# A gated mLSTM and mixture-of-experts layer: small second products queued behind other products, and four held groups of tiles in place of three

## The chip, the core and the metric

The kernel runs on one core of a Trainium2 chip. The metric is the device time of one execution in microseconds (us). Engines are named as in the profile: PE is the matrix engine, PEld its weight loads, DVE the vector engine, ACT the scalar engine, POOL the GpSimd engine, and SP the engine whose queue issues most DMA transfers. All data are fp32.

## The reference, cut to what matters

There are 8 sequences of 512 tokens, so 4096 tokens of width 1024, which the kernel cuts into 32 tiles of 128 tokens.

```python
x = x + tanh(g_xattn) * mlstm(layernorm(x), ctx, ctx, Wi, bi, Wf, bf, ln_scale)  # 16 heads of 64
x = x + tanh(g_ffn)   * ffn(layernorm(x), router_w, gate_w, up_w, down_w, shared_*)

# ffn, for T tokens of width 1024, 16 experts, the two best of each token
router_logits = flat @ router_w.T
topk_w, topk_idx = top_k(softmax(router_logits), 2);  topk_w /= sum(topk_w)
shared = (silu(flat @ shared_gate_w) * (flat @ shared_up_w)) @ shared_down_w    # hidden 1024
routed = sum over the two experts of topk_w * (silu(x @ gate_w[e]) * (x @ up_w[e])) @ down_w[e]  # hidden 512
output = shared + routed
```

In `mlstm`, an input gate and a forget gate per head come from products of the query, key and value rows with `Wi` and `Wf`. Their running sums and maxima along the sequence give a matrix of weights `d` for each head. The scores `q k` are multiplied by it, the values are summed with it, and each head is normalised.

## The kernel before

The kernel has two stages. The first goes over the 32 tiles in order. For each tile it does the attention, stores the normalised row for the experts (`y_d`, and transposed `yT_d`), routes the tile to its experts, and in between, as fill for PE, computes the shared expert of earlier tiles. The second stage runs "jobs" of up to 512 rows and a hidden width of 512: one for each of the 16 experts, and then two (the two halves of the hidden width of 1024) for each *held* group of four tiles. Held tiles are the last `4 * HELD` tiles, whose shared expert is left to the second stage. A job there multiplies in Winograd's form, seven products of quarter blocks in place of eight (`Step`, `down_tiles`), which the fill of the first stage does not.

**The loop of the first stage** (`for i in range(1, NT)`) prepares tile i + 1 while it finishes tile i and the rows of tile i - 1. On PE it issues, in the order of the program: transposes of the queries of tile i + 1 (`prep_queries`, tile `qT`), the first half of the scores of tile i (`scores(i, 0)`), transposes of the keys (`prep_keys`), fill, the gate products of tile i + 1 (`prep_gates`), the second half of the scores (`scores(i, 1)`), fill, half of the values, transposes of the finished rows of tile i - 1 (`turn_rows`), fill, router products of tile i - 1 (`finish_route`), the rest of the values, the growth of the state (`grow`), a small transpose (`prep_columns`), and fill. The first four tiles of the loop differ only in the share of fill.

**Two-step products.** `in_groups` spreads a narrow product over four groups of 32 columns of the array (tile `pp`), ACT copies the result to SBUF (tile `parts`, line 413), and a second product with the constant `sums` adds the four groups: tile `pg` (line 451) for the gates, tile `pl` (line 687) for the router. PE cannot start the second product before the copy is done.

**After pg** comes a chain for tile i + 1: ACT copies `f` (line 458), DVE works through about fifteen small operations with three visits to ACT (lines 459 to 488, ending in `nm`), and SP stores `nm` and `e` to memory and reads them back broadcast, as `d` (1 MB) and `eb` (512 KB). POOL cuts `d` to a triangle (line 522), DVE takes `decay` from `eb` (line 528) and scales `eb`, and ACT takes the exponentials of `d` (line 564), which the scores of the next turn of the loop are multiplied with (line 580). The row norms (`row_stats`, `inverse_deviation`, `normed`) go from DVE to POOL, which computes the inverse deviation (`rstd`, lines 114 and 117), and back to DVE (`row`, line 418).

**Routing.** Tiles are routed in groups of four (the last four in groups of 2, 1 and 1). When the last tile of a group has its logits, `route_group` makes one-hot rows on DVE (`hot`, `both`, `upto`), has PE add them up over the partitions (tile `pn`, lines 731 to 733, the "rank products"), computes the slots on DVE (`slots_i`, line 755), and has POOL write the eight columns of row numbers to a table in memory with indirect DMAs (line 758).

**Fill.** `shared_units` cuts the shared expert of a pair of tiles into 12 units: 8 chunks of the hidden width (line 247, 16 products of 256 columns) and 4 projections down (line 263, 8 products of 512 columns). `fill(n)` adds n to what is owed and issues whole units until the debt is paid. Weights for a chunk (two tiles of 512 KB) are streamed by SP two units ahead. From the fifth tile on, each of the four calls of a turn asks for

```python
each = (6 * (NT - 4 * HELD) - 1 - 3 * FIRST - RESERVE) / (4 * (NT - 1 - FIRST))
```

with NT = 32, FIRST = 4 and RESERVE = 8: the units of the tiles that are not held, spread over the loop, with 8 kept for the end of the stage. With HELD = 3 this is 0.917.

**Order on the engines.** The program is traced in this order, and a scheduler then builds the queue of each engine from it, by the program's order and what it takes to be ready. Each engine works off its queue in order. `tc.issue_after(ins)` keeps what is traced under it behind `ins` in the queue of the engine of `ins`, without a wait of its own.

Of the kernel before, what the change touches and what calls it, by code (L numbers as in the profile page):

```python
# [23 lines left out]
NE = 16  # L24
F = 512
NS = S // P
NC = D // P
# [5 lines left out]
MAIN = 512  # L33
REST = 64
PAIRS = 5
HELD = 3
SINGLE = 2
RESERVE = 8
FIRST = 4
# [3 lines left out]
def flamingo_layer(  # L43
# [20 lines left out]
    nc = tc.nc  # L64
    B = x.shape[0]
    T = B * S
    NT = T // P
# [135 lines left out]
    units: deque[Unit] = deque()  # L203

    owed = 0.0

    def fill(n: float = 1):
        nonlocal owed
        owed += n
        while owed > 1e-6 and units:  # L210
            unit = units.popleft()
            owed -= unit.cost
            unit.ready()
            for k in range(min(2, len(units))):
                units[k].ready()
            unit.run()
        if not units:
            owed = 0.0

    def shared_units(tiles, near=None):  # L220

        st: dict = {}
        n = len(tiles) * P

        def load_y():
            if near is not None:
                st["yT"] = near
                return
            st["yT"] = sh.tile([P, NC, 2 * P], F32, tag="yT2", name="sh_yT")
            for t, i in enumerate(tiles):  # L230
                nc.sync.dma_start(
                    st["yT"][:, :, t * P : (t + 1) * P], yT_d[i].rearrange("p (c t) -> p c t", t=P)
                )

        def load_chunk(k: int):
            if k == 0:
                load_y()
            st[k] = stream(k)

        def chunk(k: int):  # L240
            if k == 0:
                st["hT"] = sh.tile([P, 2 * NFC, 2 * P], F32, tag="hT2", name="sh_hT")
            wg, wu = st.pop(k)
            pg = ps.tile([P, 2, 2 * P], F32, tag="g", name="pgu")
            for half, w in enumerate((wg, wu)):
                for c in range(NC):
                    nc.tensor.matmul(  # L247
                        pg[:, half, :n], lhsT=w[:, c, :], rhs=st["yT"][:, c, :n],
                        start=(c == 0), stop=(c == NC - 1),
                    )  # L250
            act = sh.tile([P, 2 * P], F32, tag="act", name="sh_act", bufs=2)
            nc.scalar.activation(act[:, :n], pg[:, 0, :n], AF.Silu)
            nc.vector.tensor_mul(st["hT"][:, k, :n], act[:, :n], pg[:, 1, :n])

        def load_row(t: int):
            st["row", t] = sh.tile([P, D], F32, tag="base", name="sh_base", bufs=2)
            nc.sync.dma_start(st["row", t], x1_d[tiles[t]])

        def project_down(t: int, half: int):
            cols = slice(half * 512, (half + 1) * 512)  # L260
            po = ps.tile([P, 512], F32, tag="o", name="pso")
            for k in range(2 * NFC):
                nc.tensor.matmul(  # L263
                    po, lhsT=st["hT"][:, k, t * P : (t + 1) * P], rhs=sh_down[:, k, cols],
                    start=(k == 0), stop=(k == 2 * NFC - 1),
                )
            row = st["row", t]
            nc.vector.scalar_tensor_tensor(row[:, cols], po, tgf, row[:, cols], ALU.mult, ALU.add)
            if half == 1:
                nc.sync.dma_start(acc_d[tiles[t] * P : (tiles[t] + 1) * P, :], row)  # L270

        cost = len(tiles) / 2
        us = [Unit(lambda k=k: chunk(k), lambda k=k: load_chunk(k), cost) for k in range(2 * NFC)]
        for t in range(len(tiles)):
            us.append(Unit(lambda t=t: project_down(t, 0), lambda t=t: load_row(t)))
            us.append(Unit(lambda t=t: project_down(t, 1)))
        return us

    early = ExitStack()
    sh = early.enter_context(tc.tile_pool(name="sh", bufs=1, side="right"))  # L280
# [17 lines left out]
    with ExitStack() as actx:  # L298
# [37 lines left out]
        before_p = ac.tile([P, P], F32, name="before_p")  # L336
# [107 lines left out]
            q.kT = wk.tile([P, NC, P], F32, tag="kT", name="kT")  # L444
            transposed(q.kT, lambda c: q.kv[:, c * P : (c + 1) * P], [nc.vector.tensor_copy] * 2)

        def prep_gates(i: int):
            q, last, first = toks[i], i % NS == NS - 1, i % NS == 0
            parts = in_groups(wgt, lambda c: (q.qT if c < NC else q.kT)[:, c % NC, :], 2 * NC)
            pg = ps.tile([48, P], F32, tag="tr", name="pg")  # L450
            nc.tensor.matmul(pg, lhsT=sums, rhs=parts, start=True, stop=True)

            def row(name, bufs=2):
                return gt.tile([NH, P], F32, tag=name, name=name, bufs=bufs)
# [111 lines left out]
        def scores(i: int, g: int):  # L566

            q = toks[i]
            banks = [ps.tile([P, 4, P], F32, tag="a", name="psc") for _ in range(2)]
            for k in range(8):  # L570
                h = 8 * g + k
                lanes = slice((h % 2) * DH, (h % 2 + 1) * DH)
                nc.tensor.matmul(
                    banks[h % 2][:, k // 2, :], lhsT=q.kT[lanes, h // 2, :],
                    rhs=q.qT[lanes, h // 2, :], start=True, stop=True,
                )
            d = q.d.rearrange("p (h a) s -> p a h s", a=2)
            for hh in range(2):
                half = d[:, hh, 4 * g : 4 * g + 4, :]
                q.scored = nc.vector.scalar_tensor_tensor(  # L580
                    half, banks[hh], DH**-0.5, half, ALU.mult, ALU.mult
                ).ins

        def values(i: int, g: int):

# [5 lines left out]
            for k in range(2):  # L591
                c = 2 * g + k
                if not first:
                    nc.tensor.matmul(
                        pav[:, 2 * k : 2 * k + 2, :].rearrange("p a e -> p (a e)"),
                        lhsT=q.eb[:, c, :], rhs=state[:, c, :], start=True, stop=False,
                    )
                for hh in range(2):
                    h = 2 * c + hh
                    nc.tensor.matmul(  # L600
                        pav[:, 2 * k + hh, :], lhsT=q.d[:, h, :], rhs=q.v[:, h, :],
                        start=first, stop=first or hh == 1,
                    )
            heads = slice(4 * g, 4 * g + 4)
            nc.scalar.copy(q.u[:, heads, :], pav)
            nc.scalar.activation(q.sq[:, heads, :], pav[:, :, 0:DH], AF.Square)

        def grow(i: int):

# [70 lines left out]
                tiles = [i] if alone else [i - 1, i]  # L680
                units.extend(shared_units(tiles, near=yT if i == 0 else None))

        def finish_route(i: int):
            q = toks[i]
            parts = in_groups(rwT, lambda c: q.yT[:, c, :], NC)
            pl = ps.tile([P, NE], F32, tag="o", name="pl")
            nc.tensor.matmul(pl, lhsT=parts, rhs=sums[:, 0:NE], start=True, stop=True)
            r = group_of(i)
            k = i - r.first
            nc.vector.tensor_copy(r.logits[:, k, :], pl)  # L690
# [22 lines left out]
        def route_group(first: int):  # L713
# [3 lines left out]
            n = r.n  # L717
# [9 lines left out]
            upto = uptos[first // 4 % 2]  # L727
            for k in range(n):
                nc.vector.tensor_add(upto[:, k + 1, :], upto[:, k, :], both[:, k, :])
            pn = ps.tile([P, n + 1, NE], F32, tag="o", name="pn")  # L730
            nc.tensor.matmul(pn[:, :n, :], lhsT=before_p, rhs=both, start=True, stop=False)
            nc.tensor.matmul(pn[:, :n, :], lhsT=ones_p, rhs=upto[:, :n, :], start=False, stop=True)
            nc.tensor.matmul(pn[:, n, :], lhsT=ones_p, rhs=upto[:, n, :], start=True, stop=True)
            pos = sm.tile([P, n, NE], F32, tag="pos", name="pos", bufs=2)
# [51 lines left out]
        with tc.issue_after(normed.last):  # L786
            prep_gate_weights()
            prep_values(0)
        prep_gates(0)
        prep_columns(0)  # L790
        with tc.issue_after(normed.last):
# [12 lines left out]
        finish_rows(0)  # L804
        prep_queries(1)
        prep_keys(1)
        prep_gates(1)
        grow(0)
        turn_rows(0)
# [4 lines left out]
        load_x(2)  # L814
        prep_columns(1)
        load_kv(2)
        finish_route(0)
        fill()
        prep_norm(2)

        each = (6 * (NT - 4 * HELD) - 1 - 3 * FIRST - RESERVE) / (4 * (NT - 1 - FIRST))
        waiting: deque[int] = deque()
        for i in range(1, NT):
            nxt, last, back = i + 1 < NT, i % NS == NS - 1, i > 1
            share = 0.75 if i <= FIRST else each
# [7 lines left out]
            if back:  # L833
                head_norm(i - 1)
            fill(share)
            if nxt:
                prep_gates(i + 1)
            if waiting and i > 4:
                route_slots(waiting.popleft())
            if i == NT - 2:  # L840
                gather_table()
            scores(i, 1)
            if back:
                finish_rows(i - 1)
            if i + 2 < NT:
# [7 lines left out]
                turn_rows(i - 1)  # L853
            fill(share)
            if back:
                whole = finish_route(i - 1)
            values(i, 2)
            values(i, 3)
            head_scale(i)
            if not last:  # L860
                grow(i)
# [3 lines left out]
                prep_columns(i + 1)  # L865
            fill(share)
            if back and whole:
                g = group_of(i - 1)
                route_group(g.first)
                if g.n < 4:  # L870
                    waiting.extend(range(g.first, g.first + g.n))
            if i + 2 < NT:
                prep_norm(i + 2)
        head_norm(NT - 1)
        finish_rows(NT - 1)
        fill()
        while waiting:
            route_slots(waiting.popleft())
        turn_rows(NT - 1)
        finish_route(NT - 1)  # L880
        fill()
        route_group(NT - 1)


        key, at = (ac.tile([P, NE], F32, name=x) for x in ("key", "at"))
# [549 lines left out]
```

## Time and profile before

| | us |
|---|---|
| median of 3 runs | 3223.81 |
| lowest and highest run | 3217.66, 3227.07 |
| the profiled execution, own time | 3228.06 |
| its span, first to last instruction | 3226.3 |
| PE busy | 3104.0 (96%) |
| DVE busy | 1809.1 (56%) |
| POOL busy | 1299.9 (40%) |
| ACT busy | 862.6 (27%) |
| first product of the second stage | at 1459.68 |

A row of the timeline gives the start, the duration, the engine, the line and operation, the tiles written and read, and the count of merged instructions; in brackets stands how long the engine sat idle before it and what ended that. One fp32 product shows as two MATMUL records in most groups. A row of the stages' view gives the stretch, its length, the busy time of PE, PEld, DVE, ACT and POOL with the number of instructions, the granted PE clock as a share of full speed, the share of DMA time and GB/s. A row of the waits gives the waiting engine and line, the releaser, and then the total, the number and the longest.

### The profile page before, as it was taken

The numbers are of one execution on the slowest core, as the hardware profiler recorded it, in microseconds if no ns is written. First come the engines' busy times: TensorE is split into PE (matmuls) and PEld (weight loads), VectorE is DVE, ScalarE is ACT, GpSimd is POOL, SyncE is SP. The second block draws the span as 40 slices with busy tenths as digits, with TensorE's granted clock in tenths as the row PEclk, the third lists the DMA queues.
The fourth block names the chain that finished last, engine by engine and source line by source line (L and its number), as shares of the span: only waits on it lengthen the run. The fifth ranks groups of instructions, "written<-read, shape, count | busy, mean of one in ns | idle before, by whom it ended". The sixth has DMA issues, their size and how long they took to land.

```text
span 3226.3 us, 42288 instructions
## 1 busy us (share of the span) xinstructions
PE 3104.0 (96%) x16127; PEld 2285.2 (71%) x16127; DVE 1809.1 (56%) x3573; ACT 862.6 (27%) x1823; POOL 1299.9 (40%) x993
## 2 busy tenths in 40 slices
PE   6899989999989999999999999999999999999999
PEld 5778677686767768666666666666677777776666
DVE  5666666756667776644444444444454444456554
ACT  3434444443544544311111111111111111100000
POOL 2212232323222323226555555555565544444332
PEclk7999999999999999999999999999999999999999
DMA  6776565666646666554444554444454444645330
GB/s 196 200 229 182 172 177 177 178 182 183 204 138 195 182 200 177 167 188 147 129 114 133 140 134 128 114 128 129 130 139 137 138 129 138 183 164 176 105 131 27
DMA packets 371278, 501.50 MB, mean 155 GB/s; under 512 B 24352, under 2 KB 262480, under 8 KB 366944
## 3 DMA queue, kind: packets, MB, share of 16 engines
q1 hardware_dynamic: 342560, 425.00, 42.0%
q0 software_dynamic: 24752, 72.44, 10.8%
q8 instruction: 130, 2.13, 0.3%
q10 hardware_dynamic: 3760, 1.31, 0.2%
q14 instruction: 76, 0.62, 0.1%
HBM read 394.57 MB, written 114.61 MB: 158 GB/s over the span
## 4 chain that ended last, share of the span: by engine, by line
PE 51%; DVE 3%; issue 0%; DVEq 0%
PE pq L1237 48%; PE ptx L1155 2%; PE pq L1338 1%; DVE hsum L1301 1%; DVE hsum L1302 1%; DVE hT L1259 1%; DVE up L1258 0%; DVE tsum L1186 0%; DVE tsum L1183 0%; DVE tsum L1184 0%; DVE yo L1312 0%; DVE hT L1303 0%; DVE u L1319 0%; DVE u L1318 0%; DVE xT L1158 0%
## 5 line engine op out<-in xcount | busy, mean ns | idle before, releaser
L1237 PE MATMUL pq<-xT,w 128*128 128x256 f32 (+1 forms) x2112 | 514.1, 393 | 8.3 <-DVEq L1218 8.3
L1237 PEld LDWEIGHTS pq<-xT,w 128*128 128x128 f32 x2112 | 402.2, 191 | 101.4 <-issue 13.4
L1237 PE MATMUL pq<-tsum,wsum 128*128 128x256 f32 (+1 forms) x1408 | 349.8, 391 | 0.0
L1237 PEld LDWEIGHTS pq<-tsum,wsum 128*128 128x128 f32 x1408 | 264.0, 190 | 49.5
L247 PE MATMUL pgu<-sh_yT,swg 128*128 128x256 f32 (+1 forms) x1280 | 294.8, 381 | 0.3 <-DMA swg<-L_ffn_shared_gate_w_dram 0.3
L263 PE MATMUL pso<-sh_down,sh_hT 128*128 128x512 f32 x640 | 288.5, 602 | 0.0
L247 PE MATMUL pgu<-sh_yT,swu 128*128 128x256 f32 (+1 forms) x1280 | 276.2, 369 | 1.2 <-DMA swu<-n_L_ffn_shared_up_w_dram 1.2
L1261 DVE TENSOR_TENSOR hT<-pq,u 128x256 f32<-128x256 f32 (+1 forms) x176 | 77.3, 439 | 322.6 <-PE pq L1237 320.3
L247 PEld LDWEIGHTS pgu<-sh_yT,swu 128*128 128x128 f32 x1280 | 233.8, 190 | 31.3 <-DMA swu<-n_L_ffn_shared_up_w_dram 1.6
L247 PEld LDWEIGHTS pgu<-sh_yT,swg 128*128 128x128 f32 x1280 | 232.2, 195 | 31.7 <-issue 1.5
L114 POOL TENSOR_SCALAR ve<-bmv 128x1 f32<-128x1 f32 x64 | 15.4, 241 | 566.1 <-DVE bmv L126 553.9
L1202 POOL TENSOR_TENSOR wsum<-w 128x512 f32<-128x512 f32 x88 | 113.5, 1290 | 296.9 <-PE pq L1237 291.9
L263 PEld LDWEIGHTS pso<-sh_down,sh_hT 128*128 128x128 f32 x640 | 119.9, 193 | 134.9 <-issue 132.8
L1258 DVE TENSOR_TENSOR up<-pq,u 128x256 f32<-128x256 f32 (+1 forms) x176 | 77.2, 439 | 223.6 <-PE pq L1237 222.2
L1237 PE MATMUL pq<-wd,hT 128*128 128x512 f32 x352 | 169.6, 597 | 7.0 <-DVE hT L1259 5.4
L968 POOL DMA_INDIRECT acc_d<-yo,row_i x64 | 102.1, 1595 | 183.2 <-ACT yo L1330 70.4
L1237 PE MATMUL pq<-tsum,w 128*128 128x256 f32 (+1 forms) x704 | 174.8, 391 | 0.0
L1237 PE MATMUL pq<-xT,wsum 128*128 128x256 f32 (+1 forms) x704 | 174.8, 391 | 0.0
L1262 ACT ACTIVATE hT<-hT 128x256 f32<-128x256 f32 (+1 forms) x176 | 75.4, 428 | 341.7 <-DVE hT L1261 330.1
L1237 PE MATMUL pq<-dsum,hsum 128*128 128x512 f32 x352 | 165.4, 592 | 0.0
L1237 PE MATMUL pq<-dsum,hT 128*128 128x512 f32 x352 | 165.4, 592 | 0.0
L1312 DVE TENSOR_TENSOR yo<-pq,u 128x512 f32<-128x512 f32 x176 | 118.9, 686 | 77.1 <-PE pq L1237 56.7
(265 smaller groups left out, 5477.1 us busy)
## 6 DMA issues: line engine op xcount, KB each, us to landing
swg<-L_ffn_shared_gate_w_dram SPq DMA_DIRECT2D x88, 512.0 KB
swu<-n_L_ffn_shared_up_w_dram SPq DMA_DIRECT2D x88, 512.0 KB
w<-in_L_ffn_gate_w_dram SPq DMA_DIRECT2D x16, 2048.0 KB
w<-in_L_ffn_up_w_dram SPq DMA_DIRECT2D x16, 2048.0 KB
wd<-in_L_ffn_down_w_dram SPq DMA_DIRECT2D x16, 2048.0 KB
d<-nm_d SPq DMA_DIRECT2D x31, 1024.0 KB
x_sb<-in_x_dram SPq DMA_DIRECT2D x32, 512.0 KB
kv<-in_ctx_dram SPq DMA_DIRECT2D x32, 512.0 KB
```

What stands on the lines that cost most here:

```text
L247: nc.tensor.matmul(pg[:, half, :n], lhsT=w[:, c, :], rhs=st["yT"][:, c, :n], start=(c == 0), stop=(c == NC - 1),)
L263: nc.tensor.matmul(po, lhsT=st["hT"][:, k, t * P : (t + 1) * P], rhs=sh_down[:, k, cols], start=(k == 0), stop=(k == 2 * NFC - 1),)
L968: nc.gpsimd.indirect_dma_start(out=rows, out_offset=bass.IndirectOffsetOnAxis(ap=index, axis=0), in_=row, in_offset=None, compute_op=ALU.add,)
L1155: nc.tensor.transpose(pt[:, c, :], row[:, (half * 4 + c) * P : (half * 4 + c + 1) * P], ident)
L1202: nc.gpsimd.tensor_tensor(s1, a21, a22, ALU.add)
L1237: nc.tensor.matmul(out, lhsT=left[:, c, :], rhs=right[:, c, :], start=(c == 0), stop=(c == chunks - 1))
L1258: nc.vector.tensor_tensor(up, part, other, ALU.add)
L1259: nc.vector.tensor_tensor(out, out, up, ALU.mult)
L1261: nc.vector.tensor_tensor(out, part, other, ALU.add)
L1262: nc.scalar.activation(out, out, AF.Silu)
L1301: nc.vector.tensor_tensor(s1, a21, a22, ALU.add)
L1312: nc.vector.tensor_tensor(rows[t][:, halves[half]], part, other, ALU.add)
```

## The change

Second products are queued behind other products. `prep_gates` and `finish_route` are each cut in two: the first part (`gate_products`, `route_products`) issues the spread product and the copy, and the second part, with `pg` or `pl`, is called after the second half of the scores, or after the last quarter of the values, and pinned behind the last product of it. The second part of `route_group` becomes `place_group`; it is called in the next turn of the loop, after that turn's first fill, and its first rank product is pinned behind the last product of that fill. `HELD` goes from 3 to 4, so 16 tiles are held in place of 12, and `each` falls to 0.694. The calls at the end of the loop follow suit.

```diff
-HELD = 3
+HELD = 4
...
+    behind: list = []
...
-            unit.run()
+            behind[:] = [unit.run()]
...
+    def pinned(stack, ins):
+
+        if ins:
+            stack.enter_context(tc.issue_after(ins[0]))
...
-        def prep_gates(i: int):
+        def gate_products(i: int):
+            q = toks[i]
+            q.parts = in_groups(wgt, lambda c: (q.qT if c < NC else q.kT)[:, c % NC, :], 2 * NC)
+
+        def prep_gates(i: int, after=()):
             q, last, first = toks[i], i % NS == NS - 1, i % NS == 0
-            parts = in_groups(wgt, lambda c: (q.qT if c < NC else q.kT)[:, c % NC, :], 2 * NC)
             pg = ps.tile([48, P], F32, tag="tr", name="pg")
-            nc.tensor.matmul(pg, lhsT=sums, rhs=parts, start=True, stop=True)
+            with ExitStack() as order:
+                pinned(order, after)
+                nc.tensor.matmul(pg, lhsT=sums, rhs=q.parts, start=True, stop=True)
...
+        def finish_route(i: int, after=()):
+            q = toks[i]
             pl = ps.tile([P, NE], F32, tag="o", name="pl")
-            nc.tensor.matmul(pl, lhsT=parts, rhs=sums[:, 0:NE], start=True, stop=True)
+            with ExitStack() as order:
+                pinned(order, after)
+                nc.tensor.matmul(pl, lhsT=q.parts, rhs=sums[:, 0:NE], start=True, stop=True)
...
+        def place_group(first: int, after=()):
...
             pn = ps.tile([P, n + 1, NE], F32, tag="o", name="pn")
-            nc.tensor.matmul(pn[:, :n, :], lhsT=before_p, rhs=both, start=True, stop=False)
+            with ExitStack() as order:
+                pinned(order, after)
+                nc.tensor.matmul(pn[:, :n, :], lhsT=before_p, rhs=both, start=True, stop=False)
...
             fill(share)
+            if group is not None:
+                place_group(group, behind)
...
             if nxt:
-                prep_gates(i + 1)
+                gate_products(i + 1)
+            scored = scores(i, 1)
+            if nxt:
+                prep_gates(i + 1, scored)
...
             if back:
-                whole = finish_route(i - 1)
+                route_products(i - 1)
             values(i, 2)
-            values(i, 3)
+            valued = values(i, 3)
+            if back:
+                whole = finish_route(i - 1, valued)
...
             if back and whole:
-                g = group_of(i - 1)
-                route_group(g.first)
...
+                group = group_of(i - 1).first
+                route_group(group)
```

`scores`, `values` and the units of the fill return their last product, so that others can be pinned behind it. In the changed file the lines move: the copy is line 421, `pg` 464, `pl` 707, `pn` 760, `slots_i` 784, the indirect DMAs 787, `row` 426, `nm` 501.

## The prediction

> **What bounds the kernel now.** I read the page's forty slices first, then the stages, then the timeline of PE in the first stage and its waits, and the chain of waits for the second stage.
>
> ```profile
> PE   6899989999989999999999999999999999999999
> ```
>
> PE is busy in both stages, so both cost what PE does plus its gaps. The stages' view shows the difference (two 200 us stretches of the first stage, one of the second; after the busy times comes the PE clock):
>
> ```profile
> 400.00:600.00 200.00, 189.57 (x1354) 151.95 (x1353) 137.71 (x311) 93.49 (x210) 59.30 (x49) 0.97 0.62 180
> 800.00:1000.00 200.00, 185.57 (x1308) 147.52 (x1303) 138.58 (x295) 90.88 (x201) 52.56 (x45) 0.97 0.63 185
> 1600.00:1800.00 200.00, 200.00 (x751) 130.75 (x751) 98.90 (x166) 32.95 (x55) 107.11 (x78) 1.00 0.47 129
> ```
>
> In the first stage PE idles 10 to 14 us in 200 and loses 3% of its clock, and DVE is busy 69%. In the second there is no slack on PE. The chain of waits has the second stage's last jobs, the halves of held groups:
>
> ```profile
> 2759.82 66.64 PE pq L1237 x262
> 2833.36 66.64 PE pq L1237 x262
> ```
>
> From one start to the next is 73.54 us, which is the price of one such job.
>
> The waits of PE name what is idle in the first stage:
>
> ```profile
> PE pg L451 <- ACT parts L413: 11.3, 13, 2.9
> PE pg L451 <- issue: 8.3, 2, 4.9
> PE pl L687 <- ACT parts L413: 6.7, 4, 3.6
> PE pn L731 <- DVE both L726: 5.3, 2, 3.8
> PE pn L732 <- DVE upto L729: 3.8, 4, 2.2
> ```
>
> These five are what the pins aim at: 35.4 us. The timeline gives the rhythm, the starts of pg in two successive turns, and three pieces of fill:
>
> ```profile
> 563.87 0.42 PE L451 MATMUL pg<-parts,sums 128*48 128x128 f32 x2 [0.31 <-ACT parts L413]
> 601.10 0.42 PE L451 MATMUL pg<-parts,sums 128*48 128x128 f32 x2 [1.84 <-ACT parts L413]
> 614.21 7.03 PE L263 MATMUL pso<-sh_down,sh_hT 128*128 128x512 f32 x16
> 646.47 3.72 PE L247 MATMUL pgu<-sh_yT,swg 128*128 128x256 f32 x16
> 650.02 3.62 PE L247 MATMUL pgu<-sh_yT,swu 128*128 128x256 f32 x16
> ```
>
> A unit of fill, chunk or projection, is 7.0 us of PE. From the pg at 265.84 to the one at 1323.84 there are 25 turns, 42.3 us each on average. Counting the fill rows between them, 17 turns have four units and take 44.1 us in the mean, 8 have three and take 38.5.
>
> **The change part by part.**
>
> *Second stage.* Two more jobs at 73.5 us: **+147**. Job lengths do not vary (both rows above read 66.64), and the stretch holding them shows DMA busy 51%, so I keep ±3.
>
> *Fill.* Four tiles are two pairs of 12 units; 24 units leave the first stage. At 7.0 us they are 168 us of PE, 21 more than the two jobs cost: that is the whole gain of the Winograd form. But a turn with one unit less is only 5.6 us shorter (44.1 - 38.5), because the fill covers gaps. At that rate 24 units are **-134**.
>
> *Lost cover beyond that.* The changed order asks for 3 units in about half the turns and 2.3 to 2.9 in the rest, where before it was 3 or 4. At 2.78 a turn PE needs some 13.9 us for attention (the turns' lengths less fill and idle) plus 19.5, so 33.4. DVE's share of 42.3 us is 28.9; less its small part in 0.9 unit it is 28.4. To it come waits that are DVE's own: POOL's rstd, 0.8 to 1.0 us twice a turn, and ACT's returns in the gate chain, 1.3 to 2.1. That is 32 to 33 us. And in the turns of 36 to 39 us the chain from pg over nm and eb's landing to the next pg already fills most: decay starts 26 to 28 us after pg, and 9 to 12 us of work follow before the next pg. Three resources stand within 2 us of each other. I take 1 us a turn over 25 turns, **+25**, between 0 (PE alone sets the pace) and 3 us a turn (+75).
>
> *Pins.* If all five waits go, PE gains 35.4 us, and clock with them. A piece of the timeline shows both, and what the long ones have in common:
>
> ```profile
> 436.88 0.27 ACT L413 COPY parts<-pp 128x128 f32<-128x128 f32 x1 [4.30 <-remote]
> 437.20 0.42 PE L451 MATMUL pg<-parts,sums 128*48 128x128 f32 x2 [3.38 <-issue]
> 438.92 0.97 POOL L758 DMA_INDIRECT table_d<-rowid,slots_i  x1 [0.30 <-issue]
> 440.86 0.81 DVE L418 TENSOR_SCALAR row<-x_sb,bmv,rstd 128x1024 f32<-128x1024 f32 x1 [6.79 <-issue]
> 441.82 0.45 PE L400 MATMUL pt<-ident,row 128*128 128x128 f32 x1 [3.39 <-DVE row L418]
> ```
>
> The four pg waits of 2.8 us and more (at 265.8, 437.2, 775.8, 1278.8) all lie in or at the end of POOL's burst of eight indirect DMAs, which takes about 10.5 us (429.12 to 439.9 here) and comes seven times. ACT starts the copy late there although its product is done; the trace calls it remote and does not say why. The pin moves pg from behind 2 to 4 of the second-half scores to behind all 8. The eight take 1.16 us together, so the pin alone covers 0.9 us at most: enough for waits of 0.31, not of 3.
>
> *The clock, row against rule.* After such gaps the clock reads
>
> ```profile
> 440.00:450.00 10.00, 8.18 (x36) 7.93 (x37) 4.30 (x12) 5.79 (x10) 0.74 (x2) 0.50 0.40 107
> 770.00:780.00 10.00, 7.09 (x58) 4.08 (x57) 6.29 (x11) 0.68 (x3) 6.52 (x8) 0.83 0.28 62
> ```
>
> The Trainium skill, "TensorE: Matmul & The Clock Gate", in the section on the HAM clock gate, says that PE falls to half clock after an idle window of about 3.4 us. It speaks against thinning the fill. By its rule only the waits near or over 3.4 us cost clock; among the pinned ones that is four, at one window of half clock each, 4 x 1.7 = 7 us. The second row shows clock lost (0.17 x 10 = 1.7 us) with no wait over 2.9, so here shorter ones suffice. Adding (1 - clock) x 10 us over the slices after pinned waits gives about 20. I take the trace: the pinned waits cost 35 + 20 = 55; by the rule it is 42, and the sum below would be 13 higher. I book **-55**, all gone: pl waits out some 2 us more of values, pn a whole fill, and the burst moves away from pg. If only the short waits go, it is -15.
>
> *Where the burst goes.* That move has a price. place_group now runs after the next turn's first fill, so DVE makes slots_i two or three operations after pg's first readers. In the changed POOL queue, all seven times, the rstd for the finished rows of tile i - 1 stands behind the eight DMAs. In the changed DVE queue, line 426, which needs that rstd, comes 1 to 14 operations after slots_i, mostly in the middle of the gate chain, ahead of nm. The operations between take 1 to 8 us, the burst 10.5: DVE stands still for 2.5 to 10 us, some 35 us over seven bursts. Queued behind it are the rest of the gate chain, so nm, then SP's stores and reloads of d and eb, then ACT's exponentials; PE waits for the same row in turn_rows, after 8 to 12 us of values and fill. Before, this happened twice (the 6.79 above, and 5.50 at 1279.55). The nearest price is the turn that began at 437.2 with three units: nm came 19.1 us after pg, where 10 to 15 is usual, and it took 43.2 us where the other seven take 37.8: 5.4, rounded up to 6 as fill is thinner. Seven times: **+42**; between +15 (fill hides it) and +60.
>
> *At nothing:* the queue of SP, which loses 16 chunk loads of 1 MB and does not gain an issue in the first stage; the end of the stage, which keeps its reserve of 8 units; the copies to the output, 4 issues for 5, beside the last jobs. If the cover of these were gone, 5 us.
>
> Sum: 147 - 134 + 25 - 55 + 42 = **+25**. Against the profiled execution's 3228.1 that is 3253; it stands 4.3 us above the median, so 3249 as a median. A measurement of this kernel tells about 0.3% (10 us) from no change.
>
> **The rivals.**
>
> *A, faster: the cover is enough.* If PE alone sets the pace and the burst is hidden: 147 - 168 - 55 + 15 = -61 at best. With half the loss of cover (-151 in place of -134) and a burst at +20: -39, so **3185**. For it: no idle of over 1 us on PE, apart from what the pins aim at, in five of the eight turns with three units. Against it: those turns stood between turns of four units, in which DVE caught up (8 to 19 us idle), and these neighbours go.
>
> *B, much slower: the gate chain becomes the bound.* If nm is late in every turn after a burst, and pg, eb and decay then set the pace at 38 us or more, lost cover is +60 to +75: **3290**. It decides once the chain from pg to pg exceeds PE's 34 us by over 2 us on average.
>
> *C, the pins do not do what they say.* If ACT's late copy is not due to the burst, the 0.9 us leaves most of the pg waits: 15 us gained in place of 55, so +65, **3289**. It joins B's range.
>
> **How the numbers follow.** Forecast, +10 to +75 with 3249 likeliest: 0.45. A, -10 to -76: 0.30. B and C, mostly above +60: 0.15. Within 10 us, where A's and the forecast's terms cancel: 0.10. So faster 0.30, same 0.10, slower 0.60. The range leaves out the outer quarter of A and half of B and C: 3178 to 3302. The forecast's own range is 3234 to 3299.
>
> **What would show it.** Right: pg, pl and pn wait for under 10 us together; line 426 waits on POOL several us in each burst; turns average about 38 us; the second stage starts near 1340 in place of 1459.7, and has 24 jobs with the last eight at 73.5. Wrong: turns of 36 us or less with DVE never held by the burst (A); pg still waiting 3 us on ACT outside a burst (C); turns of 40 us and cold clock in most slices (B).

## The result, and the profile after

The changed kernel takes 3271.43 us (median of six runs, 3260.81 to 3273.35) against 3222.41 for the one before: ratio 1.0138, 95% interval [1.0122, 1.0155], slower by about 1.4%. (The ratio is not the plain quotient of the two medians, which is 1.0152; it comes to 44 us where the medians stand 49 apart.) The forecast, slower and 3249, has the right sign and holds the time in its range, but about half of the loss is missing from it: +25 was forecast, +49 came. The profiled spans stand at 3226.3 and 3268.8, +42.5.

The forty slices and the stages' view (columns as before: busy times, then PE clock, DMA share, GB/s) show where:

```profile
PE   6899999989899989899999999999999999999999
```

```profile
400.00:600.00 200.00, 184.91 (x1339) 145.98 (x1338) 145.93 (x326) 100.58 (x229) 65.12 (x57) 0.95 0.61 180
800.00:1000.00 200.00, 187.61 (x1374) 145.81 (x1373) 145.10 (x329) 100.53 (x224) 57.21 (x50) 0.98 0.60 184
1400.00:1600.00 200.00, 200.00 (x763) 133.51 (x762) 98.33 (x165) 29.77 (x51) 108.11 (x78) 1.00 0.45 124
```

In the first stage PE idles 12 to 15 us in 200, where it idled 10 to 14 before, and in the first of the two stretches it has 0.95 of its clock instead of 0.97 (0.98 in the second). The second stage has no gaps, and now covers the stretch at 1400. It starts at 1355.29 (first `pq` in PE's timeline; 1459.68 before): the first stage is 104.4 us shorter. From there to the end it is 1913.5 us, where it was 1766.6: 146.9 longer. The chain of waits has the added jobs, at the old price of 73.5 us from start to start:

```profile
2654.79 66.64 PE pq L1281 x262
2728.34 66.64 PE pq L1281 x262
2801.87 66.64 PE pq L1281 x262
```

So the whole question lies in the first stage, which had to shrink by more than 147 and did not. PE's waits there (us in total, times, longest), one row of before and then after:

```profile
PE pt L400 <- DVE row L418: 27.6, 9, 9.5
```

```profile
PE pt L408 <- DVE row L426: 56.1, 12, 9.3
...
PE pt L408 <- DMA kv<-in_ctx_dram: 9.7, 3, 4.2
...
PE pl L707 <- ACT parts L421: 3.5, 4, 2.0
```

The waits of pg, pl and pn that the pins aim at were 35.4 us; pl's 3.5 and 0.7 of pg are left, and pn no longer waits. In their place stands one row above all: the transposes in `turn_rows` wait for `row` (line 426, 418 before), 56.1 us where it was 27.6. A burst turn's timeline says why, in order of time from the turn's pg on. By a burst I mean the eight indirect writes of one group; a turn that holds the middle of one is a burst turn.

```profile
1018.04 0.42 PE L464 MATMUL pg<-parts,sums 128*48 128x128 f32 x2
1024.11 1.11 POOL L787 DMA_INDIRECT table_d<-rowid,slots_i  x1 [12.23 <-DVE slots_i L784]
...
1033.41 0.97 POOL L787 DMA_INDIRECT table_d<-rowid,slots_i  x1 [0.30 <-issue]
...
1034.75 0.57 POOL L117 TENSOR_TENSOR rstd<-ve,mhalf 128x1 f32<-128x1 f32 x1
1035.36 0.81 DVE L426 TENSOR_SCALAR row<-x_sb,bmv,rstd 128x1024 f32<-128x1024 f32 x1 [6.45 <-POOL rstd L117]
1036.22 1.97 PE L408 MATMUL pt<-ident,row 128*128 128x128 f32 x8 [5.45 <-DVE row L426]
1039.34 0.21 DVE L501 TENSOR_SCALAR nm<-m 16x128 f32<-16x128 f32 x1
```

The eight writes hold POOL for 10.3 us. The rstd behind them is late, DVE stands 6.45 us for it, PE 5.45 us for DVE, and `nm`, the end of the gate chain, comes 21.3 us after pg. I split the 25 turns from pg 263.80 to pg 1226.84 by whether a burst falls in them, adding up PE's waits in the timeline and the stretches at half clock:

| turns | before | after |
|---|---|---|
| all 25: us each, units of fill | 42.3, 3.7 | 38.5, 2.8 |
| without a burst | 41.8 (19) | 35.9 (18) |
| with a burst | 43.9 (6) | 45.4 (7) |
| PE's waits, a turn without / with a burst | 1.2 / 4.4 | 1.7 / 6.8 |
| half clock, a turn without / with a burst | 2.3 / 1.3 | 2.1 / 7.9 |

A turn without a burst became 6 us shorter. A turn with one became longer, and now costs 9.5 us more than its neighbours.

The 25 turns together became 95 us shorter (1058.0 to 963.0), and their parts add up. PE has 22.8 units of fill less, by its rows. But it waits 78 us where it waited 48, and it runs 92 us at half clock (the 0.50 of the stages' view) where it ran 51, which at half speed is another 20 us. So about 50 us of what the thinner fill saves is lost again, two fifths of it as clock.

### The profile page after: what moved, and what is told of

The parts are those of the page before. It is cut to its first block, busy times and chain, and to the rows that moved or that the text cites. A ratio compares the mean times of both kernels' runs of the same rounds, so it can differ in the third digit from the quotient of the medians.

```text
span 3268.8 us, 42389 instructions
## 1 busy us (share of the span) xinstructions
PE 3113.5 (95%) x16047; PEld 2289.3 (70%) x16047; DVE 1842.8 (56%) x3677; ACT 856.8 (26%) x1828; POOL 1365.5 (42%) x1033
## 4 chain that ended last, share of the span: by engine, by line
PE 54%; DVE 4%; issue 0%; DVEq 0%
PE pq L1281 52%; PE ptx L1199 2%; DVE hsum L1345 1%; PE pq L1382 1%; DVE hsum L1346 1%; DVE hT L1303 1%; DVE up L1302 0%; DVE tsum L1230 0%; DVE tsum L1227 0%; DVE tsum L1228 0%; DVE yo L1356 0%; DVE hT L1347 0%; DVE u L1363 0%; DVE u L1362 0%; DVE xT L1202 0%
## 5 line engine op out<-in xcount | busy, mean ns | idle before, releaser
L1281 PE MATMUL pq<-xT,w 128*128 128x256 f32 (+1 forms) x2304 | 557.5, 392 | 8.9 <-DVEq L1262 8.9
L1281 PEld LDWEIGHTS pq<-xT,w 128*128 128x128 f32 x2304 | 438.2, 191 | 107.6 <-issue 23.5
L1281 PE MATMUL pq<-tsum,wsum 128*128 128x256 f32 (+1 forms) x1536 | 380.1, 390 | 0.0
L1281 PEld LDWEIGHTS pq<-tsum,wsum 128*128 128x128 f32 x1536 | 288.3, 190 | 52.8
L248 PE MATMUL pgu<-sh_yT,swg 128*128 128x256 f32 (+1 forms) x1024 | 251.5, 390 | 0.6 <-DVE sh_hT L254 0.6
L265 PE MATMUL pso<-sh_down,sh_hT 128*128 128x512 f32 x512 | 239.0, 614 | 0.6 <-ACT sq L620 0.6
L248 PE MATMUL pgu<-sh_yT,swu 128*128 128x256 f32 (+1 forms) x1024 | 219.6, 367 | 1.0 <-DMA swu<-n_L_ffn_shared_up_w_dram 1.0
L248 PEld LDWEIGHTS pgu<-sh_yT,swg 128*128 128x128 f32 x1024 | 185.0, 201 | 28.3 <-issue 6.2
L248 PEld LDWEIGHTS pgu<-sh_yT,swu 128*128 128x128 f32 x1024 | 185.0, 191 | 24.0 <-DMA swu<-n_L_ffn_shared_up_w_dram 1.1
L1335 POOL TENSOR_TENSOR dsum<-wd 128x1024 f32<-128x1024 f32 x48 | 128.2, 2882 | 138.0 <-PE pq L1281 138.0
```

Source lines behind the costliest of these rows:

```text
L248: last = nc.tensor.matmul(pg[:, half, :n], lhsT=w[:, c, :], rhs=st["yT"][:, c, :n], start=(c == 0), stop=(c == NC - 1),)
L265: last = nc.tensor.matmul(po, lhsT=st["hT"][:, k, t * P : (t + 1) * P], rhs=sh_down[:, k, cols], start=(k == 0), stop=(k == 2 * NFC - 1),)
L1281: nc.tensor.matmul(out, lhsT=left[:, c, :], rhs=right[:, c, :], start=(c == 0), stop=(c == chunks - 1))
L1335: nc.gpsimd.tensor_tensor(out, p, q, ALU.subtract)
```

## The experiments

Theory T: the burst on POOL is what the changed kernel loses by. Rival R: the fill is too thin, so that DVE and the gate chain set the pace whether there is a burst or not. Each result is a ratio to the kernel before, run beside it on the same chip; "stage two" is its start in the profiled execution. A profile is one execution, up to 15 us from its kernel's median (e6's was the fastest of ten, 14.6 below; e9's the slowest of six, 8.2 above). So the ratios and medians say what a version costs, and the profiles say where. In all profiles of twelve held tiles the rest behind it is 1765 to 1767 us, in all of sixteen 1913 to 1915, so differences are made in the first stage alone.

| run | held | ratio | stage two | turns without / with burst |
|---|---|---|---|---|
| before | 12 | 1 | 1459.7 | 41.8 / 43.9 |
| e1, pins | 12 | 0.9982 | 1445.8 | 40.7 / 45.6 |
| e7, pins, burst behind rstd | 12 | 0.9968 | 1455.2 | 40.6 / 45.7 |
| e12, pins, burst behind wv | 12 | 0.9955 | 1455.1 | 41.3 / 42.4 |
| e9, pins, table by products | 12 | 0.9949 | 1455.6 | 41.9 / none |
| after | 16 | 1.0138 | 1355.3 | 35.9 / 45.4 |
| e2, held alone | 16 | 1.0095 | 1344.5 | 36.6 / 42.6 |
| e5, rank as before | 16 | 1.0092 | 1348.2 | 36.4 / 42.9 |
| e3, burst behind rstd | 16 | 1.0061 | 1337.6 | 35.9 / 41.5 |
| e8, burst in four pairs | 16 | 1.0125 | 1359.4 | 36.4 / 43.6 |
| e11, burst behind wv | 16 | 1.0060 | 1334.6 | 37.2 / 38.5 |
| e10, table by products | 16 | 1.0032 | 1329.0 | 37.7 / none |
| e6, no burst | 16 | 0.9990 | 1296.7 | 36.1 / none |
| e13, POOL busy, no writes | 16 | 1.0167 | 1366.6 | 36.4 / 44.3 |

**The parts alone.** e1 is the changed kernel with

```diff
-HELD = 4
+HELD = 3
```

> The changed kernel with HELD back at 3: the pins and the moved rank products alone. Theory T (the loss comes from POOL's burst of eight indirect DMAs, which now stands ahead of the rstd that the row of tile i - 1 waits for, some 9 us in each of seven turns): the burst turns stay 5 to 9 us longer than the others here too, so the pins bring little, about 3200 to 3225. Rival R (the thinner fill is the cause: DVE and the gate chain set the pace once a turn has fewer than three units): with the fill back the pins bring all of the 55 us of waits that they aim at, about 3170.

Measured: 3217.78 us, 0.9982 [0.9972, 0.9993]. e2 is the kernel before with the opposite edit.

> The kernel before with HELD = 4 alone: no pins, rank products and burst at their old place. T: turns without a burst about 36 to 37 us as in the changed kernel, and a cheaper burst, so about 3230 to 3250, faster than the changed kernel. R: all of the loss is here, and no pins soften it: 3271 or more.

Measured: 3258.18 us, 1.0095 [1.0077, 1.0114], between T's range and R's. The held tiles alone carry most of the loss; the pins with the moved rank products gain 0.2% with twelve held tiles (as T says) and lose 0.4% with sixteen. PE's waits in e1's first stage show why the gain is small:

```profile
PE pt L408 <- DVE row L426: 29.1, 9, 9.3
PE pt L408 <- DMA kv<-in_ctx_dram: 10.7, 9, 3.8
...
PE pc L530 <- ACT rows L523: 5.7, 2, 5.2
PE pl L707 <- ACT parts L421: 5.5, 4, 3.2
```

pg and pn are gone from the list, 30 of the five waits' 35.4 us with them. But over the 25 turns PE's waits add up to 43.3 us against 48.0 before, and the half clock to 61 us against 51: the time that pg and pn had waited is now waited for row 426, for the keys' load and for the gate rows.

**The rank as before, behind the other pins.** e5 keeps sixteen held tiles and the pins of pg and pl, and puts the whole of `route_group` back to the end of the turn.

```diff
-                group = group_of(i - 1).first
-                route_group(group)
+                g = group_of(i - 1)
+                route_group(g.first)
+                place_group(g.first)
```

> HELD = 4 with the pins of gates and router, but route_group whole and at its old place at the end of the turn. T (the moved burst costs the difference between a burst turn and the others): this version has the old, cheaper burst, 42 to 43 us in those turns as in the run of HELD = 4 alone, and the better other turns of the changed kernel, so about 3235 to 3250. R (thin fill, the burst's place is nothing): 3265 or more, as the changed kernel.

Measured: 3263.82 us, 1.0092 [1.0061, 1.0124], as e2. That is near R's forecast, not T's: back at its old place the burst is not cheap, its turns take 42.9 against 36.4. With sixteen held tiles the pins of pg and pl bring nothing that shows, and moving the rank (with its burst) costs a further 0.5%, about 15 us (the two intervals just touch; the profiles say 7).

**No burst.** e6 drops the 56 indirect writes and nothing else.

```diff
-            for k in range(n):
-                for a in range(2):
-                    nc.gpsimd.indirect_dma_start(
...
```

> The changed kernel without the 56 indirect DMAs that write row numbers to the table; the second stage then works on rows that are not the routed ones, its amount of work is the same. T: the seven turns fall from 45 us to the 36 of the others, 60 us less: about 3205 to 3215, which is what the burst costs in all. R: those turns also carry the rank products and some 4 us of DVE work, and stay at 41 or more: 3245 or above.

Measured: 3227.28 us, 0.9990 [0.9971, 1.0009], between T's range and R's and nearer to T's. Against the changed kernel that is 48 us by the ratios; stage two starts 58.6 us earlier, in an execution that was 14.6 us under its median. The 25 turns take 36.1 us on average with 2.8 units, and PE waits 1.9 us in each. Against the changed kernel's turns (61 us shorter in all) PE waits 47 us in place of 78 and runs 34 us at half clock in place of 92, which is 32 + 29 = 61: half of what the burst costs is clock. The same ten microseconds of a turn in the stages' view, 12 to 22 us behind its pg (1018.04 after, 979.00 in e6), after and then e6:

```profile
1030.00:1040.00 10.00, 4.55 (x13) 2.75 (x12) 3.88 (x10) 2.51 (x4) 4.31 (x6) 0.77 0.32 59
```

```profile
991.00:1001.00 10.00, 10.00 (x88) 6.51 (x86) 6.55 (x20) 3.22 (x9) 2.59 (x4) 1.00 0.64 208
```

R falls as far as its pace goes: the thin fill by itself does not hold the turns at 38 us. But the burst is not the whole loss. e6 only comes level with a kernel that still has its own burst; e9 and e10 below compare twelve and sixteen held tiles with no burst on either side.

**Moving the burst.** e3 pins the eight writes behind the rstd that they had held up, e8 issues them in four pairs (behind that rstd, behind head_scale's pow, behind the next tile's mask, behind the norm's rstd), and e7 is e3 with twelve held tiles.

```diff
+            if placed is not None:
+                with tc.issue_after(toks[i - 1].rstd):
+                    write_slots(placed)
```

> The changed kernel with the eight indirect DMAs of a group called after finish_rows and pinned behind its rstd on POOL; the rank products stay where the change put them. T: line of row no longer waits on POOL for 4 to 7 us, burst turns fall from 45 to about 38 us, 7 x 7 = 50 us less: about 3221. R: the burst turns are long for want of fill, little changes: 3260 or more.

> The changed kernel with the eight DMAs in four pairs over the turn: behind the rstd of finish_rows, the scale of the heads, the cut of d and the rstd of the next norm. T: no instruction of POOL is held by more than 2.6 us, the burst turns come near 38: about 3220 to 3230. If the burst's cost is not the hold on POOL but the transfers themselves beside the stores of nm and e, spreading brings little over the version with the burst later: 3240 to 3250.

> HELD = 3 with all pins and the eight DMAs behind the rstd of finish_rows. T: the burst turns, 45.6 us with the pins alone, lose about 4 us as they did with HELD = 4 (45.4 to 41.5): 3218 - 27 = about 3190, the fastest so far. R: with full fill the burst was hidden anyhow, 3210 to 3220.

Measured: e3 3246.40 us, 1.0061 [1.0044, 1.0078]; e8 3271.11, 1.0125 [1.0097, 1.0154]; e7 3221.25, 0.9968 [0.9948, 0.9988]. e3 regains about half of what e6 does, e8 next to nothing, which no theory had; e7 came as R says, no clear gain over e1. POOL's timeline in e8, then DVE and PE, has the second price of a burst, which I had not seen in the queue:

```profile
1042.31 0.97 POOL L794 DMA_INDIRECT table_d<-rowid,slots_i  x1 [0.30 <-issue]
1043.29 1.08 POOL L629 TENSOR_TENSOR state<-state,decay 64x520 f32<-64x520 f32 x1
1052.14 1.06 POOL L629 TENSOR_TENSOR state<-state,decay 64x520 f32<-64x520 f32 x1 [7.77 <-DMA table_d<-rowid,slots_i]
```

```profile
1053.24 0.43 DVE L646 TENSOR_TENSOR state<-state,pst 64x260 f32<-64x260 f32 x1 [6.96 <-POOL state L629]
```

```profile
1053.72 3.17 PE L586 MATMUL psc<-qT,kT 64*128 64x128 f32 x16 [7.58 <-DVE state L646]
```

The second `state *= decay` waits until the writes ahead of it have landed, 8.9 us after the last was issued, though it does not touch the table; why it waits for them the runs do not show. POOL's waits in all (of e3, then of e8):

```profile
POOL state L629 <- DMA table_d<-rowid,slots_i: 23.2, 7, 4.9
```

```profile
POOL state L629 <- DMA table_d<-rowid,slots_i: 31.5, 6, 8.1
```

Before, e2 and e5, with the burst at the turn's end, have no such row; after has 9.5. So the burst must stay clear of two instructions, not one. A version that takes rstd off POOL altogether, to DVE (e4), gave no result; what that would bring is open.

**Both avoided.** e11 pins the burst behind `wv`, where POOL's longest gap begins.

```diff
+            if placed is not None:
+                with tc.issue_after(toks[i + 1].weighed):
+                    write_slots(placed)
```

> The changed kernel; the eight table writes of a group are pinned behind `wv <- v, cols` at the end of the turn, the start of POOL's longest gap (in e6, POOL has nothing between the end of wv, 5.5 us ahead of the turn's pg, and the rstd of row 426, 6.5 us behind it). T (what a burst costs is the POOL instruction that it is in the way of): it starts 7 us ahead of pg, ends 3 us behind it, its last write lands near 12 us behind it, ahead of the second `state *= decay` (14 us behind it), so neither the rstd nor state waits: burst turns about 37, near 3232, ratio 1.000 to 1.003. R (the writes cost about 6 us a burst wherever they are, by their DMA traffic and by being there): as e2 and e5, near 3262, ratio 1.009.

> The same with HELD = 3. T: burst turns, 45.6 in e1 against 40.7 in the others, come down to about 41: up to 7 x 4.9 = 34 us less than e1, near 3190 to 3200, ratio 0.990 to 0.993, a version ahead of both kernels. R: nothing gained over e1, ratio 0.997 to 0.998.

Measured: e11 3249.86 us, 1.0060 [1.0038, 1.0082]; e12, the same with twelve, 3216.13, 0.9955 [0.9940, 0.9969]. e12 lies between T and R. In e11 the mechanism came as T says: state waits for a landing once, 1.3 us, and burst turns fell to 38.5. The time did not. The burst lies across a pg here, and its cost went to the turn that follows: the turns after the one in which a burst begins take 40.1 us, where the same turns of e6 take 37.0. The burst took 12.6 us in the turn I looked at (1030.51 to 1043.12, three writes 1.6 to 2.0 us long in place of 0.97), longer than planned, and the rstd of row 426 began right behind it at 1043.15. e11 ends no faster than e3, and neither theory had that. It stays 22 us behind e6 by the medians (38 by the profiles, of which some 35 lie in the 25 turns). Nearly all of these are clock and waits on PE: 78 us at half clock in place of 34, which at half speed is 22, and 58 us of waits in place of 47. Why a burst that holds up neither rstd nor state for long still brings them I did not settle.

**POOL busy, nothing written.** e13 puts in place of the writes as much POOL time without a transfer.

```diff
+            for k in range(8):
+                idle = sm.tile([P, 5], F32, tag="idle", name="idle")
+                nc.gpsimd.tensor_tensor(idle, late, mhalf[:, 0:5], ALU.pow)
```

> The changed kernel with the eight table writes of a group replaced, at the same place of POOL's queue and behind the same slots, by one add and eight pow operations of 128 x 5 elements into a scratch tile (by the rows of rstd, 0.57 us for one element, and hrstd, 2.91 us for sixteen, about 1.2 us each, some 10 us in all, against 10.3 for the writes). Nothing is transferred and nothing lands; the table stays zero, so the output is not the reference's. T1 (what costs is that POOL is held for 10 us ahead of rstd): burst turns near 44 to 45, the 3271 of the changed kernel less the 5 to 10 us that state waits for landings, 3261 to 3271, ratio 1.010 to 1.014. T2 (what costs is the writes' traffic and landing, which e11's place could not avoid): near e6, 3227 to 3240, ratio 0.999 to 1.003. Between, 3245 to 3255: both, in the proportion that it shows.

Measured: 3281.99 us, 1.0167 [1.0141, 1.0193]: the whole loss of the changed kernel (the intervals overlap), with no table write in it. POOL's timeline, and DVE's waits for the first stage, after and then e13 (e6 has 47.5):

```profile
1030.56 9.10 POOL L789 TENSOR_TENSOR idle<-late,mhalf 128x5 f32<-128x5 f32 x8
1039.64 0.22 POOL L114 TENSOR_SCALAR ve<-bmv 128x1 f32<-128x1 f32 x1
1039.94 0.57 POOL L117 TENSOR_TENSOR rstd<-ve,mhalf 128x1 f32<-128x1 f32 x1
```

```profile
DVE row L426 <- POOL rstd L117: 75.0, 54, 7.5
```

```profile
DVE row L426 <- POOL rstd L117: 92.7, 56, 9.2
```

At the changed kernel's place, ten busy microseconds of POOL ahead of rstd are enough to explain what the burst costs there; the writes' traffic is not needed for it.

**The table without POOL.** e9 (twelve held) and e10 (sixteen) build the table with one-hot products, one tile a turn, as the kernel before does for its last four tiles only.

```diff
-                    nc.gpsimd.indirect_dma_start(
...
+            for t in due[:1]:
+                make_slots(t)
```

> HELD = 3, all pins, and no indirect write of the table at all: the table is built by two one-hot products and an add for every tile (one tile a turn, in route_slots' place), as the kernel before does only for the last four tiles, and the gather of the table falls away. The output is the whole one. T (the burst of eight indirect DMAs on POOL costs about 5 us in each of seven turns even with twelve held tiles: burst turns 45.6 against 40.7 in e1): 34 us less than e1 (3217.8), and back 28 tiles x 0.55 us of products = 15: about 3199, ratio 0.991; all turns near 41.2. R (the burst is hidden while fill is thick, turns are set by the fill and the gate chain): no gain, 3217.8 + 15 = 3233, ratio 1.002.

> The changed kernel with the same replacement of the indirect writes by products. The output is the whole one. T: as e6 (3227.3, no burst, table left out) plus 28 x 0.55 = 15 us of products, less a few us for the gather: about 3240, ratio 1.003; turns near 36.6, none of them long, second stage near 1310. So sixteen held tiles stay behind twelve (e9) by about 40 us even with no burst: the second stage's two jobs cost more than the fill saves. R (thin fill: each product more that waits for DVE stands open): turns 38 or more, about 3275, ratio 1.014.

Measured: e9 3214.50 us, 0.9949 [0.9933, 0.9965]; e10 3241.58, 1.0032 [1.0020, 1.0045]. e10 came as T says. e9 gains, but less than the 0.991 of T: its turns take 41.9, not 41.2, so in the profile, the slowest of its six runs, the products and their preparation cost what the burst had; its lead over e1 is across two sets of runs. e9 and e12 are ahead of both kernels, by half a per cent, and both hold twelve tiles. In one set of runs e10 stands 27 us behind e9: even with no burst, sixteen held tiles lose, since the fill that leaves saves 120 us (147 - 27) and not 147. That part of the loss lies in the trade itself and not in the burst.

## Why the prediction was right, and where its sum was not

*Second stage, +147.* Measured 146.9. The price of a job, read off two rows of the chain, held in every run.

*Fill -134 and lost cover +25, together -109.* Without a burst in either, e10's second stage starts 126.6 us earlier than e9's (120 by the medians). With the burst at its old place, e2's starts 115.2 earlier than before's. The discount of a thinner fill was a little too pessimistic; the turns came to 35.9 us between bursts, where 38 was feared. The 33.4 us of PE in a turn came out: e6's 36.1, less 1.9 of waits and 0.7 of lost clock, is 33.5. The reading that a unit is worth 5.6 us and not its 7.0 was the important one: at 7.0 these terms would have made the change a gain (147 - 168).

*Pins, -55.* This is the step that failed. "If all five waits go, PE gains 35.4 us, and clock with them": in e1 30 us of them went, and its stage two starts only 13.9 us earlier, 0.2% or 6 us in the runs. With sixteen held tiles the pins of pg and pl brought nothing (e5 against e2). A wait that ends last on PE is not time that PE gets back if another engine is due just behind it. In e1 row 426, the keys' load and the gate rows took the place, PE's waits in the 25 turns fell by 4.7 us, and no clock was won (61 us at half clock, 51 before). The 20 us booked for clock from the trace, and the 13 less by the rule, are then both beside the point; in the changed kernel about as much clock was lost instead. Part of e1's gain is eaten by its own moved burst (turns with one 43.9 to 45.6), so with twelve held tiles the pins by themselves are worth somewhat more than the 6 to 14.

*Where the burst goes, +42.* Right in place and mechanism, too large as the price of the move. DVE waited for POOL in all seven bursts, by 1.5 to 7.5 us; `nm` came 19 to 22 us after pg in the last four, and burst turns cost 9.5 us over their neighbours. Removing the burst gives 48 us by the ratios. But moving it cost only about 15 (after against e5), because at its old place it already costs 6.5 us a turn once the fill is thin (42.9 against 36.4 in e5). The prediction had read the old place as nearly free, off turns with full fill, where a burst costs 2.0 us; and of the bursts that held DVE up before it named two and passed over a third (3.60 us at 778.18).

*The sum.* The prediction's steps can be taken one at a time, each as a pair of versions (medians, each against the kernel before beside it):

| step | booked | measured |
|---|---|---|
| sixteen held tiles (e2) | 147 - 134 + 25 = +38 | +34 |
| pins of pg and pl (e5 against e2) | 26.3 of the 35.4 us: -41 | 0 |
| rank and burst moved, pn pinned (after against e5) | 42 - 14 = +28 | +15 |
| all | +25 | +49 |

The split of the -55 between pg and pl and pn is by their waits, an estimate; the last two steps hold only within what sets of runs scatter, some 10 us. So the sign was no luck: the first step carries it, and its terms were right. That the total stayed inside the range owes something to chance: the pins, booked 41 too high, were offset in part by a move booked 13 too dear.

*The rivals.* A, the cover is enough and the burst hidden (3185): of the cover about a third, since fill and cover came at -120 to -127, between the booked -109 and A's -151; and e6 shows what a hidden burst would have been worth. Even so e6 is only level with the kernel before, since A's -55 for the pins was not to be had. B, the gate chain at 38 us or more in every turn: no, 35.9 in turns without a burst. C, the pins leave pg waiting for ACT: no, pg waits 0.7 us; it was the waits' worth, not the waits, that stayed away. Of the signs named, pg, pl and pn under 10 us (4.2) and turns of about 38 us (38.5) came out; line 426 waited several us in five bursts of the seven (1.5 and 1.7 in the others); and the second stage, expected near 1340, started at 1355, 15 us late.

## What to carry to other kernels

Before a wait is booked as a gain, look who is due next at the same engine: with 30 us of waits gone, e1 was 6 us faster by the medians (14 by the profiles), because row, keys and gate rows came no earlier than before. A burst's price read off turns with much fill does not hold for turns with little. Moving work that is itself off the path to another place of an engine's queue has a price of its own, and the length of the burst and every instruction behind it (also waits on its landing) are what to count; try the extreme, no burst at all, and the same time with no transfer, before moving it about. And a trade of fill for a shorter algorithm must be reckoned with what a unit of fill costs in a turn (5.6 here), not with its own duration (7.0).

## What the runs showed of the hardware that was not expected

A write of the burst, 128 words to scattered places, takes POOL about 1.28 us from one to the next (0.97 of it busy; up to 2.3 in the burst of e11), and a POOL instruction that waited for the last one of a pair began 8.9 us after its issue (e8, above).

The clock fell to half after waits much shorter than in the case that the prediction weighed. In e11, PE's timeline and the stages' view (the clock is the third from the last):

```profile
874.18 1.13 PE L586 MATMUL psc<-qT,kT 64*128 64x128 f32 x8 [0.57 <-DVE state L646]
876.58 2.04 PE L586 MATMUL psc<-qT,kT 64*128 64x128 f32 x8 [1.27 <-DVE state L646]
```

```profile
873.00:878.00 5.00, 3.16 (x18) 2.61 (x17) 4.80 (x11) 4.15 (x11) 4.38 (x2) 0.83 1.12 270
878.00:883.00 5.00, 5.00 (x14) 3.88 (x14) 3.40 (x3) 3.61 (x9) 4.53 (x4) 0.50 0.13 51
```

Two waits of 0.57 and 1.27 us with little between them, 1.84 idle in 5, went with half clock: 0.83 in the first row puts its start some 1.7 us before 878 (0.17 x 5 / 0.5), about when the second wait ended, and it lasts through the five microseconds of the second row. The rule that the prediction quotes from the Trainium skill, "TensorE: Matmul & The Clock Gate", of an idle window of about 3.4 us, does not foresee that; the measurement decides.
